# A graph layer on one core: the first four tiles' adjacency scanned ahead of the table of rows, and the table's loads and stores issued by GpSimd

## The chip, the cores and the metric

The kernel runs on one core of a Trainium2 chip. A core has five engines with instruction queues of their own: TensorE (PE in the profile; PEld is its loading of weights), VectorE (DVE), ScalarE (ACT), GpSimd (POOL) and SyncE (SP). Each engine takes its instructions in the order that was fixed before the run. Transfers between memory and the core are issued from the queues of SP, ACT and POOL and are carried by 16 DMA engines. The metric is the device time of one execution in microseconds (us), and the time of a kernel is the median of its runs.

## The reference, cut to what matters

There are 4096 nodes with 128 features (`x`) and an adjacency of 4096 x 4096 integers, with about 64 neighbours per node. Layer 0 is graph attention with 8 heads; layer 1 takes quantiles over the neighbours.

```python
def _L0_gnn_ref(nodes, adj, W, a1, a2, W1, b1, gamma, beta):
    Wh = jnp.einsum('nd,hde->hne', nodes, W)
    f1 = jnp.einsum('hnd,hd->hn', Wh, a1)
    f2 = jnp.einsum('hnd,hd->hn', Wh, a2)
    e = jax.nn.leaky_relu(f1[:, :, None] + f2[:, None, :], negative_slope=ALPHA)
    mask = (adj > 0)[None, :, :]
    att = jnp.where(mask, e, jnp.float32(-9000000000000000.0))
    att = jax.nn.softmax(att, axis=-1)
    h = jnp.einsum('hnm,hmd->hnd', att, Wh)
    h = jax.nn.elu(h)
    cat = jnp.transpose(h, (1, 0, 2)).reshape(N, NHEADS * DIM)
    x = jax.nn.elu(cat @ W1 + b1)
    out = _layernorm(nodes + x, gamma, beta)
    return out

def _L1_gnn_ref(x, A, W, b):
    ...
    keep = mask & ~remove
    n_keep = keep.sum(axis=1)
    vals = jnp.where(keep[:, :, None], x[None, :, :], big)
    svals = jnp.sort(vals, axis=1)
    w_q = jnp.asarray(1.0 / len(QUANTILES), x.dtype)
    for q in QUANTILES:
        idx = jnp.maximum(jnp.ceil(q * n_keep).astype(jnp.int32) - 1, 0)
        picked = jnp.take_along_axis(svals, idx[:, None, None], axis=1)[:, 0, :]
        agg = agg + w_q * picked
    ...
```

## The kernel before

The 4096 nodes are 32 tiles of 128 rows, and the tiles are grouped into six blocks of 4, 4, 6, 6, 6 and 6. The kernel uses the sparsity: it finds each node's list of neighbours and gathers only those rows. Three kinds of work make up the first stage.

**The front** (class `Front`) turns the adjacency into lists. `scan` loads a tile's adjacency in quarters of 128 x 1024 integers (L365, issued by SP, three buffers `a_i`), ACT checks each quarter for negative values (L367) and turns it into zeros and ones (L374), and PE packs these into words (L376, `ps_words`). `first` makes keys from the words (L389, DVE) and drains them, largest eight at a time, in 13 rounds of `MAX8` and `MATCH_REPLACE8` (`drain8`, L182 and L184). `second` and a last `drain8` finish the lists of a batch of tiles. `place` sorts the nodes of a block by the number of neighbours (result `pos_i`, L505) and POOL scatters the lists to memory (L526, `rows_d`). `pieces` cuts all of this into pieces that the main function calls up with `advance(n)`; the open pieces of a block do not count. The first piece scans tile 0. The piece of tile 0 scans tile 1 and drains tile 0; the piece of tile 1 scans tiles 2 and 3 together and drains tile 1; the pieces of tiles 2 and 3 drain these.

**The table** (`table`) writes a row for every node to memory (`xf_d`): its 128 features, then 8 + 8 numbers for the heads. It loads `w`, `x` in four parts, and `a2` and `a1` copied to all partitions; DVE multiplies and reduces `a` with `w` to `wa` (L250, L251); PE transposes `x` (L138) and ACT copies the transposed blocks out (L139); 32 products with `wa`, which show as 64 matmuls (L254), make the numbers of the heads, and ACT copies them out (L255). Four stores (L257) write the table. Its on-chip memory is a pool that is closed when the function returns.

**The gathers** (`gat`). Behind the table `gat` opens pools of its own and loads its constants (L802 to L810); DVE fills two small rows of padding (L813, stored by L814) and makes small selection tiles (L819 to L825). `load(u)` then gathers the table's rows of the neighbours for half a tile (L886, POOL) with the lists that `place` scattered (read back at L842 and L847); `load(0)` first runs all pieces through the placing of block 0. Attention, projections and normalisation of one tile after the other follow, with `advance(2)` behind each half tile, and the new rows go to memory (L1094).

The second stage (`sparse`) gathers these rows (L1549) and sorts them on DVE (L1584, L1585).

The program is written in one order, but the order on each engine is made by a scheduler before the run: it goes by the order of the program as priority and takes a later instruction first where it expects the earlier one not to be ready. So instructions of the front stand among those of the table. An instruction whose memory is freed by a pool that was closed waits for the last use of that memory.

Of the kernel before, what the change touches and what calls it, by code (L numbers as in the profile page):

```python
# [38 lines left out]
F32 = mybir.dt.float32  # L39
# [7 lines left out]
AX = mybir.AxisListType  # L47
# [3 lines left out]
P = 128  # L51
N = 4096
D = 128
NT = N // P
H = 8
# [76 lines left out]
def transpose_all(nc, psum, out, blocks, ident):  # L132

    for i in range(0, len(blocks), 4):
        ps = psum.tile([P, 4, P], F32, name="ps_tr")
        n = len(blocks[i : i + 4])
        for j in range(n):
            nc.tensor.transpose(ps[:, j, :], blocks[i + j], ident)  # L138
        nc.scalar.copy(  # L139
            out[:, i * P : (i + n) * P], ps[:, :n, :].rearrange("p a b -> p (a b)")  # L140
        )
# [79 lines left out]
    return wf, base  # L221


def table(tc, nc, c, x, w, a1, a2, xf_d):

    with tc.tile_pool(name="ta", bufs=1) as tp, tc.tile_pool(
        name="ta_ps", bufs=2, space=PSUM
    ) as psum:
        w_sb = tp.tile([P, H, D], F32, name="w_ta")
        nc.scalar.dma_start(out=w_sb, in_=w.rearrange("h d e -> d h e"))  # L230
        pad = tp.tile([1, XF], F32, name="pad_x")
        nc.gpsimd.memset(pad, 0.0)
        nc.gpsimd.memset(pad[:, D : D + H], -BIG)
        nc.scalar.dma_start(out=xf_d[0:1, :], in_=pad)
        xf = tp.tile([P, NT, XF], F32, name="xf")
        for i in range(4):
            nc.scalar.dma_start(
                out=xf[:, ts(i, 8), :D],
                in_=x[ts(i, 1024), :].rearrange("(t p) d -> p t d", p=P),
            )  # L240
        xT = tp.tile([P, N], F32, name="xT_ta")
        transpose_all(nc, psum, xT, [xf[:, t, :D] for t in range(NT)], c["idf"])
        wa = tp.tile([P, 2 * H], F32, name="wa_ta")
        for i, a in enumerate((a2, a1)):
            abc = tp.tile([P, H, D], F32, name="abc_ta", bufs=2)
            nc.scalar.dma_start(
                out=abc.rearrange("p h e -> p (h e)"),
                in_=a.rearrange("h e -> (h e)").partition_broadcast(P),
            )
            nc.vector.tensor_mul(abc, abc, w_sb)  # L250
            nc.vector.reduce_sum(wa[:, ts(i, H)], abc, axis=AX.X)  # L251
        ps_f = psum.tile([P, NT, 2 * H], F32, name="ps_fa", bufs=1)
        for t in range(NT):
            nc.tensor.matmul(ps_f[:, t, :], xT[:, ts(t, P)], wa, start=True, stop=True)  # L254
        nc.scalar.copy(xf[:, :, D:], ps_f)  # L255
        for i in range(4):
            nc.scalar.dma_start(  # L257
                out=xf_d[1 + i * 1024 : 1 + (i + 1) * 1024, :].rearrange(
                    "(t p) d -> p t d", p=P
                ),  # L260
                in_=xf[:, ts(i, 8), :],
            )
# [494 lines left out]
def gat(tc, nc, c, x, adj, xf_d, meta_d, order_d, flag_d, w, a1, a2, w1, b1, gamma, beta, x1_d):  # L757
# [22 lines left out]
    with ExitStack() as ctx:  # L780
# [3 lines left out]
        def advance(count):  # L784
            while todo and count > 0:
                name, piece = todo.pop(0)
                piece()
                count -= name != "open"
# [4 lines left out]
                advance(1)  # L793

        advance(1)
        table(tc, nc, c, x, w, a1, a2, xf_d)
        one = ctx.enter_context(tc.tile_pool(name="ga1", bufs=1))
        tp = ctx.enter_context(tc.tile_pool(name="ga2", bufs=2))
        rowp = ctx.enter_context(tc.tile_pool(name="ga3", bufs=6))
        psum = ctx.enter_context(tc.tile_pool(name="ga_ps", bufs=1, space=PSUM))  # L800
        w_sb = one.tile([P, H, D], F32, name="w_ga")
        nc.scalar.dma_start(out=w_sb, in_=w.rearrange("h d e -> d h e"))  # L802
        w1_sb = one.tile([P, H, D], F32, name="w1_ga")
        nc.scalar.dma_start(out=w1_sb, in_=w1.rearrange("(h e) o -> e h o", e=D))
        b1_sb = one.tile([P, 1], F32, name="b1_ga")
        nc.scalar.dma_start(out=b1_sb, in_=b1.rearrange("(o k) -> o k", k=1))
        bc = {}
        for name, src in (("gamma", gamma), ("beta", beta)):
            bc[name] = one.tile([P, D], F32, name=f"{name}_ga")
            nc.scalar.dma_start(out=bc[name], in_=src.partition_broadcast(P))  # L810
        for row, value in PADS:
            pad = one.tile([1, D], F32, name="pad", bufs=2)
            nc.vector.memset(pad, value)  # L813
            nc.scalar.dma_start(out=x1_d[row : row + 1, :], in_=pad)  # L814


        small = front.small[:, max(BLOCKS) * NC :]
# [286 lines left out]
        e, _ = probabilities(0, held[0], f1s[0])  # L1104
        going = []
        zT = None
        for u in range(2 * NT):
# [6 lines left out]
            if u + 1 < 2 * NT:  # L1114
                with ExitStack() as order:
                    for ins in behind:
                        order.enter_context(tc.issue_after(ins))
                    e, behind = probabilities(u + 1, held[u + 1], f1s[(u + 1) // 2])
# [912 lines left out]
def gnn(tc, x, adj, w, a1, a2, w1, b1, gamma, beta, lw, lb, out):  # L2031
    nc = tc.nc
    with ExitStack() as ctx:
        dram = ctx.enter_context(tc.tile_pool(name="dram", bufs=1, space=DRAM))
        xf_d = dram.tile([N + 1, XF], F32, name="xf_d")
        x1_d = dram.tile([N + len(PADS), D], F32, name="x1_d")
        meta_d = dram.tile([N, MW], I32, name="meta_d")
        order_d = dram.tile([N, 1], I32, name="order_d")
        flag_d = dram.tile([1, 1], I32, name="flag_d")

        keep = ctx.enter_context(tc.tile_pool(name="keep", bufs=1))
        c = constants(nc, keep)
        gat(tc, nc, c, x, adj, xf_d, meta_d, order_d, flag_d, w, a1, a2, w1, b1, gamma, beta, x1_d)
        other = nc.values_load(flag_d[0:1, 0:1], min_val=0, max_val=1)
        with tc.If(other > 0) as cmp:
            general(tc, nc, c, x, adj, w, a1, a2, w1, b1, gamma, beta, lw, lb, x1_d, out)
        with cmp.Else():
            sparse(tc, nc, c, x1_d, meta_d, order_d, lw, lb, out)
# [36 lines left out]
```

## Time and profile before

| | us |
|---|---|
| median of 3 runs | 8008.65 |
| lowest, highest | 8007.93, 8008.86 |
| profiled execution, its own time | 8009.1 |
| its span in the trace | 8007.3 |
| POOL busy, share of the span | 4407.1, 55% |
| DVE busy, share of the span | 5869.6, 73% |
| first gather of the table's rows starts | 179.2 |
| first gather of the second stage starts | 3244.0 |

The page divides the span into 40 slices of 200 us and shows the busy share of each engine as a digit in tenths. Lines of groups read: line, engine, operation, out<-in with shapes, count, then busy time and mean ns of one, then the engine's idle time just before them and what ended it. Lines of the timeline begin with the start and the duration; what stands in brackets is the idle time before and its releaser. Lines of waits read: what waited, for what, then us in total, times, longest.

### The profile page before, as it was taken

To read this page: it belongs to the slowest core of one execution; us is meant where nothing else is said; L and a number is where in the kernel's file an instruction comes from. 1 tells how busy PE (TensorE), PEld (TensorE's weight loads), DVE (VectorE), ACT (ScalarE), POOL (GpSimd) and SP (SyncE) were. 2 spreads that over 40 slices of the span, in tenths; PEclk is the share of its full clock that TensorE was granted. 3 is DMA by queue.
4 is the path that set the end of the run, shared out by engine and by line. 5 is a ranking of instruction groups with operands and counts; after the bars stand their busy time and mean duration, and the time that the engine had idled before them with its cause. 6 is when DMAs were issued, how large, how long until landed. Compare 5 with 4: busy or idle time off the path is not lost. (4 is left out here: it accounts for less than half of the span.)

```text
span 8007.3 us, 29926 instructions
## 1 busy us (share of the span) xinstructions
PE 1005.5 (13%) x5587; PEld 841.1 (11%) x5587; DVE 5869.6 (73%) x9452; ACT 2152.7 (27%) x2120; POOL 4407.1 (55%) x4564
## 2 busy tenths in 40 slices
PE   3233323322222322100000000000000000000000
PEld 1222222222222222000000000000000000000000
DVE  6555556555222222399889999999988999999999
ACT  5021202100000000133333333333333333333333
POOL 1777777777777776645435353635445444554500
PEclk9766666666566665555555555555555555555555
DMA  6232424222222222111101010101111011111100
GB/s 186 60 101 75 113 62 117 60 56 52 51 56 56 56 56 52 44 31 39 33 26 37 26 39 26 42 24 38 30 29 36 25 29 30 37 34 27 34 1 1
DMA packets 222575, 385.09 MB, mean 48 GB/s; under 512 B 121637, under 2 KB 133416, under 8 KB 222376
## 3 DMA queue, kind: packets, MB, share of 16 engines
q0 software_dynamic: 145664, 305.55, 16.1%
q1 hardware_dynamic: 64258, 70.19, 2.9%
q10 hardware_dynamic: 12454, 7.34, 0.3%
q14 instruction: 153, 1.25, 0.1%
q8 instruction: 46, 0.75, 0.0%
HBM read 372.47 MB, written 10.31 MB: 48 GB/s over the span
## 5 line engine op out<-in xcount | busy, mean ns | idle before, releaser
L1549 POOL DMA_INDIRECT rows<-x_d,info x2078 | 2037.5, 981 | 2055.4 <-DVE agg L1632 1040.5
L886 POOL DMA_INDIRECT nb<-xf_d,ids x2250 | 2139.8, 951 | 698.1 <-issue 662.6
L1583 ACT COPY low<-rows 128x2048 f32<-128x2048 f32 (+9 forms) x1009 | 1548.2, 1551 | 2552.2 <-DVE rows L1585 2210.8
L1584 DVE TENSOR_TENSOR rows<-low,rows 128x2048 f32<-128x2048 f32 (+9 forms) x1009 | 1877.3, 1885 | 210.1 <-ACT low L1583 207.0
L1585 DVE TENSOR_TENSOR rows<-low,rows 128x2048 f32<-128x2048 f32 (+9 forms) x1009 | 1875.4, 1883 | 2.7
L962 DVE TENSOR_TENSOR e<-nb,ps_small 128x144 f32<-128x144 f32 (+8 forms) x166 | 43.4, 264 | 1313.6 <-DMA nb<-xf_d,ids 1248.0
L1008 PE MATMUL ps_z<-spread,nb 128*128 128x128 f32 x4500 | 615.5, 305 | 769.4 <-DVE spread L1001 748.2
L1008 PEld LDWEIGHTS ps_z<-spread,nb 128*128 128x128 f32 x4500 | 604.4, 220 | 803.1 <-DVE spread L1001 381.0
L1639 PE MATMUL low<-idf,com 128*128 128x128 f32 x32 | 15.2, 474 | 4704.3 <-DVE rows L1585 3839.5
L970 ACT ACTIVATE ps_e<-e 128x256 f32<-128x256 f32 (+4 forms) x64 | 26.1, 408 | 1939.0 <-DVE e L962 1854.3
L1639 PEld LDWEIGHTS low<-idf,com 128*128 128x128 f32 x32 | 5.8, 181 | 4713.6 <-DVE rows L1585 3535.3
L1001 DVE TENSOR_TENSOR spread<-e,ps_small 128x1152 f32<-128x1152 f32 (+4 forms) x312 | 342.8, 1107 | 87.5 <-PE ps_z L1008 85.0
L1646 POOL DMA_INDIRECT out<-o,info x32 | 39.8, 1243 | 506.3 <-DVE o L1645 500.5
L1583 ACT COPY low_s<-rows 128x256 f32<-128x256 f32 (+3 forms) x321 | 144.8, 470 | 397.7 <-DVE rows L1584 238.1
L367 ACT ACTIVATE nz<-a_i 128x1024 bf16<-128x1024 int32 x128 | 134.4, 1051 | 233.1 <-DMA a_i<-in_adj 191.1
L182 DVE MAX8 k<-key 128x8 f32<-128x256 f32 x416 | 165.4, 411 | 0.9
L1584 DVE TENSOR_TENSOR rows<-low_s,rows 128x256 f32<-128x256 f32 (+3 forms) x321 | 156.4, 496 | 1.4 <-ACT low_s L1583 0.7
L1585 DVE TENSOR_TENSOR rows<-low_s,rows 128x256 f32<-128x256 f32 (+3 forms) x321 | 156.4, 497 | 0.4
L184 DVE MATCH_REPLACE8 key<-k,key 128x256 f32<-128x256 f32 x384 | 155.6, 407 | 0.0
L900 DVE TENSOR_TENSOR mine<-me,group 128x64 f32<-128x64 f32 x32 | 6.8, 213 | 197.2 <-DMA me<-xf_d,info 194.1
L376 PE MATMUL ps_words<-nz,pows 128*128 128x512 bf16 (+1 forms) x272 | 111.8, 568 | 289.7 <-ACT nz L374 196.0
L1587 DVE TENSOR_TENSOR rows<-rows 128x256 f32<-128x256 f32 (+8 forms) x245 | 138.4, 578 | 0.1
(222 smaller groups left out, 2502.9 us busy)
## 6 DMA issues: line engine op xcount, KB each, us to landing
a_i<-in_adj SPq DMA_DIRECT2D x128, 512.0 KB, 4.5
nb<-xf_d,ids POOLq DMA_INDIRECT x2250
rows<-x_d,info POOLq DMA_INDIRECT x2078
xf_d<-xf ACTq DMA_DIRECT2D x4, 576.0 KB, 7.5
xf<-in_x ACTq DMA_DIRECT2D x4, 512.0 KB, 7.9
meta_d<-rowdata_k SPq DMA_DIRECT2D x4, 324.0 KB, 4.0
abc_ta<-in_L_gnn_a ACTq DMA_DIRECT2D x2, 512.0 KB, 7.3
w_ga<-in_L_gnn_W ACTq DMA_DIRECT2D x2, 512.0 KB, 4.9
```

Of the source, the lines that this page charges most:

```text
L182: nc.vector.max(out=top, in_=work)
L184: nc.vector.match_replace(out=work, in_to_replace=top, in_values=work, imm_value=gone)
L367: nc.scalar.activation(nz[:, j, :], a_i, AF.Relu, scale=-1.0, accum_out=self.negative[:, k : k + 1],)
L376: nc.tensor.matmul(ps_w[:, :m, :], self.pows[:, 4 * i + b, :], nz[:, :m, ts(b, NG1)], start=i + b == 0, stop=i + b == 6,)
L886: gather = nc.gpsimd.indirect_dma_start(out=rows[:, at + i, :], out_offset=None, in_=xf_d, in_offset=bass.IndirectOffsetOnAxis(ap=ids[:, k ...
L1001: last = nc.vector.tensor_tensor(spread[:, :m], e[:, at : at + m, :].unsqueeze(2).to_broadcast(shape), own.unsqueeze(1).unsqueeze(3).to_br ...
L1008: product = nc.tensor.matmul(ps_z[:, g, :], rows[:, k + i0 + i, :D], spread[:, i].rearrange("p j h -> p (j h)"), start=i0 + i == 0, stop=i ...
L1549: nc.gpsimd.indirect_dma_start(out=row, out_offset=None, in_=x1_d, in_offset=bass.IndirectOffsetOnAxis(ap=info[:, col : col + 1], axis=0),)
L1583: nc.scalar.copy(packed, lows)
L1584: nc.vector.tensor_tensor(lows, packed, highs, op=ALU.min)
L1585: nc.vector.tensor_tensor(highs, packed, highs, op=ALU.max)
L1587: nc.vector.tensor_tensor(lows, lows, highs, op=ALU.min)
```

## The change

In `table`, all transfers are issued by POOL in place of ACT, in the order `w`, `a2`, `a1`, the four parts of `x`, the row of padding; the stores of the table too. The tiles `abc` are loaded at the start. A function `between` is called behind the loads; `gat` passes `advance(2)`, so the pieces of tiles 0 and 1 stand there in program order: the scan of tile 1, the drains of tile 0, the scan of tiles 2 and 3, the drains of tile 1. The steps on `a` (DVE) now stand ahead of the transposes. In `gat`, the loads of the constants and the stores of the two rows of padding are issued by POOL; the memsets of L813 stay on DVE.

```diff
-def table(tc, nc, c, x, w, a1, a2, xf_d):
+def table(tc, nc, c, x, w, a1, a2, xf_d, between):
...
-        w_sb = tp.tile([P, H, D], F32, name="w_ta")
-        nc.scalar.dma_start(out=w_sb, in_=w.rearrange("h d e -> d h e"))
         pad = tp.tile([1, XF], F32, name="pad_x")
         nc.gpsimd.memset(pad, 0.0)
         nc.gpsimd.memset(pad[:, D : D + H], -BIG)
-        nc.scalar.dma_start(out=xf_d[0:1, :], in_=pad)
+        w_sb = tp.tile([P, H, D], F32, name="w_ta")
+        nc.gpsimd.dma_start(out=w_sb, in_=w.rearrange("h d e -> d h e"))
+        wa = tp.tile([P, 2 * H], F32, name="wa_ta")
+        abcs = []
+        for a in (a2, a1):
+            abc = tp.tile([P, H, D], F32, name="abc_ta", bufs=2)
+            nc.gpsimd.dma_start(
+                out=abc.rearrange("p h e -> p (h e)"),
+                in_=a.rearrange("h e -> (h e)").partition_broadcast(P),
+            )
+            abcs.append(abc)
         xf = tp.tile([P, NT, XF], F32, name="xf")
         for i in range(4):
-            nc.scalar.dma_start(
+            nc.gpsimd.dma_start(
                 out=xf[:, ts(i, 8), :D],
                 in_=x[ts(i, 1024), :].rearrange("(t p) d -> p t d", p=P),
             )
+        nc.gpsimd.dma_start(out=xf_d[0:1, :], in_=pad)
+        between()
+        for i, abc in enumerate(abcs):
+            nc.vector.tensor_mul(abc, abc, w_sb)
+            nc.vector.reduce_sum(wa[:, ts(i, H)], abc, axis=AX.X)
         xT = tp.tile([P, N], F32, name="xT_ta")
         transpose_all(nc, psum, xT, [xf[:, t, :D] for t in range(NT)], c["idf"])
-        wa = tp.tile([P, 2 * H], F32, name="wa_ta")
-        for i, a in enumerate((a2, a1)):
-            abc = tp.tile([P, H, D], F32, name="abc_ta", bufs=2)
-            nc.scalar.dma_start(
-                out=abc.rearrange("p h e -> p (h e)"),
-                in_=a.rearrange("h e -> (h e)").partition_broadcast(P),
-            )
-            nc.vector.tensor_mul(abc, abc, w_sb)
-            nc.vector.reduce_sum(wa[:, ts(i, H)], abc, axis=AX.X)
...
         for i in range(4):
-            nc.scalar.dma_start(
+            nc.gpsimd.dma_start(
                 out=xf_d[1 + i * 1024 : 1 + (i + 1) * 1024, :].rearrange(
...
         advance(1)
-        table(tc, nc, c, x, w, a1, a2, xf_d)
+        table(tc, nc, c, x, w, a1, a2, xf_d, lambda: advance(2))
...
-        nc.scalar.dma_start(out=w_sb, in_=w.rearrange("h d e -> d h e"))
+        nc.gpsimd.dma_start(out=w_sb, in_=w.rearrange("h d e -> d h e"))
...
-        nc.scalar.dma_start(out=w1_sb, in_=w1.rearrange("(h e) o -> e h o", e=D))
+        nc.gpsimd.dma_start(out=w1_sb, in_=w1.rearrange("(h e) o -> e h o", e=D))
...
-        nc.scalar.dma_start(out=b1_sb, in_=b1.rearrange("(o k) -> o k", k=1))
+        nc.gpsimd.dma_start(out=b1_sb, in_=b1.rearrange("(o k) -> o k", k=1))
...
-            nc.scalar.dma_start(out=bc[name], in_=src.partition_broadcast(P))
+            nc.gpsimd.dma_start(out=bc[name], in_=src.partition_broadcast(P))
...
-            nc.scalar.dma_start(out=x1_d[row : row + 1, :], in_=pad)
+            nc.gpsimd.dma_start(out=x1_d[row : row + 1, :], in_=pad)
```

## The prediction

> **What bounds the kernel now.** I read the slices of the page first, then the waits of GpSimd (POOL) in the stretch where it is busiest, then the first 180 us instruction by instruction.
>
> ```profile
> DVE  6555556555222222399889999999988999999999
> POOL 1777777777777776645435353635445444554500
> ```
> ```profile
> L886 POOL DMA_INDIRECT nb<-xf_d,ids x2250 | 2139.8, 951 | 698.1 <-issue 662.6
> L1584 DVE TENSOR_TENSOR rows<-low,rows 128x2048 f32<-128x2048 f32 (+9 forms) x1009 | 1877.3, 1885 | 210.1 <-ACT low L1583 207.0
> ```
>
> A slice is 200 us. From slice 2 to slice 16 POOL sits at 0.7: 2250 gathers of table rows (L886), 0.95 us each plus 0.3 us "issue" ahead of each, so 1.25 us a gather. From slice 17 DVE sorts the lists at 0.9 and is the bound to the end. The sort reads rows that the first stage wrote, so the two follow each other. The waits of POOL from 170 to 3260 us say whether anything stops the first stage:
>
> ```profile
> POOL nb L886 <- issue: 662.6, 2174, 0.3
> POOL rows_d L526 <- DVE pos_i L505: 165.7, 1, 165.7
> POOL x_d L1094 <- DVE s L1091: 45.3, 2, 40.6
> POOL x_d L1094 <- DMA x_d<-s,info: 14.8, 9, 2.0
> ```
>
> One wait stands out, 165.7 us in one piece: POOL does nothing until DVE has placed the first block of four tiles. What the kernel can win at its head is therefore won one for one at its end: first gather at 179.20, everything behind it 8007.3 - 179.2 = 7828.1 us. The head itself:
>
> ```profile
> 20.55 0.42 DVE L389 SCALAR_TENSOR_TENSOR key<-ps_words,iota_g 128x256 f32<-128x256 f32 x1 [15.99 <-PE ps_words L376]
> ...
> 60.38 0.31 DVE L813 MEMSET pad<- 1x128 f32 x2 [21.93 <-DMA xf_d<-xf]
> ...
> 66.59 0.42 DVE L389 SCALAR_TENSOR_TENSOR key<-ps_words,iota_g 128x256 f32<-128x256 f32 x1 [5.23 <-PE ps_words L376]
> ```
> ```profile
> 87.18 0.75 DVE L389 SCALAR_TENSOR_TENSOR key<-ps_words,iota_g 128x256 f32<-128x256 f32 x2 [7.90 <-PE ps_words L376]
> ```
> ```profile
> DVE key L389 <- PE ps_words L376: 29.1, 3, 16.0
> DVE pad L813 <- DMA xf_d<-xf: 21.9, 1, 21.9
> ```
>
> (Timeline, then waits of DVE in the first 180 us.) DVE starts tile 0 at 20.55, tile 1 at 66.59, tiles 2 and 3 at 87.18; between them it stands 21.9 us until the table's stores have landed (the pad of L813 lies in memory that the table's pool frees), 5.2 and 7.9 us for the scans. From 87.18 on it is busy without a break to pos_i, so 179.20 - 87.18 = 92.0 us from tiles 2 and 3 to the first gather. ACT, which makes the scans, has the same holes:
>
> ```profile
> ACT xf L255 <- PE ps_fa L254: 14.8, 1, 14.8
> ...
> ACT nz L367 <- DMA a_i<-in_adj: 10.2, 13, 1.1
> ACT nz L374 <- DMA w_ga<-in_L_gnn_W: 10.1, 1, 10.1
> ```
>
> The copy L255 waits for the table's matmuls and the load of w_ga for the stores' landing, both with scans queued behind.
>
> **The change, part by part.**
>
> *Scans ahead of the table.* Undisturbed, ACT takes four quarters in 9.33 us (activations of L367 start at 76.84 and 86.17). Sixteen quarters from 6.41 are 37.3 us, with the 16 copies of pows (3.3 us) 47.0; the last activation of tiles 2 and 3 ended 1.95 us before their key (85.23 to 87.18), so the key could start at 48.9. The transfers bound it too: 16 quarters of 0.52 MB and the loads of w, a and x (3.7 MB) are 12.1 MB, at 236 GB/s (the rate of 0 to 20 us, DMA share 0.78) 51 us. I take 50. DVE is ready: tiles 0 and 1 take 12.7 us each (66.59 to 79.3), 20.55 + 25.4 = 46. The four DVE steps of L250 and L251 (4.8 us) fit into its idle time before 20.55 if w and a have landed, otherwise they cost up to 4.8 here. Gain if nothing else holds DVE: 87.2 - 50 = **37 us**.
>
> *The issues leave ACT.* ACT spent about 17 us issuing (w 0.46, x 4.6, a 2.6, pads 1.1, stores 5.0, w_ga to beta 3.2) and the 10.1 us wait for w_ga; both are inside the 37 us. On POOL the waiting costs nothing as long as its first scatter comes late: behind the stores POOL has w_ga, w1_ga and five small ones, at most 2 x 7.9 + 5 x 1.25 = 22 us, and the scatter comes over 80 us after the pad. That cover is what hides them.
>
> *What a plain transfer costs on POOL.* The trace has none. Nearest is the gather, 128 rows in 0.95 us. A load of x or w or a store of xf_d has 1024 rows. If the cost is per instruction it is 1.25 us with its issue; if per row 8 x 0.95 + 0.3 = 7.9 us. I take the middle, 4.5, since the gather has the same row length (544 against 576 bytes) but eight times fewer rows. x's last load is then issued at about 27 us (low end 11, high end 44) and lands 7.9 us later, the rows' own figure. At the high end transposes placed among the scans hold these up some 10 us.
> The Trainium skill, "DMA: Bandwidth & Descriptors", section "Anatomy of one DMA — SWDGE (gpsimd) path", calls descriptor generation small, with many descriptors emitted before the added cost shows. By that the low end holds and the 13 us that I charge below for late stores would be nothing, the time of rival A; no run shown has a transfer of more than 128 rows on this queue.
>
> *The wait at L813 stays.* The pads' memsets are still on DVE, still in memory that the table frees, and they still stand ahead of first(2) in program order. Which drains DVE does before them depends on the scheduler: in the trace it filled first(0) in ahead of L813, because that was ready earlier. So what is late next is the stores' landing. The table: eight copies of xT (0.58 us) and 64 matmuls (13.8 us in a row). If the copies go into ACT's waits for a_i (0.8 us each), L255 comes at about 50; if all wait for the scans, 47.0 + 8 x 0.87 + 13.8 = 68. I take 58. Four stores of 4.5 us and 7.5 us landing (the page's figure for xf_d): 58 + 18 + 7.5 = **83.5**; ends 50 + 5 + 7.5 = 62.5 and 68 + 31.6 + 7.5 = 107.
> DVE reaches L813 somewhere in the drains of tiles 2 and 3, 25 us long (87.18 to 112). The order is fixed before the run, by when the scheduler expects the stores. I assume that it expects the chain that I do but the price per instruction: 58 + 5 + 7.5 = 70.5, so 20.5 us into the drains. DVE then stands 83.5 - 70.5 = 13 us.
> The skill's "SBUF — State Buffer", section "SBUF: two separate sides", speaks against the change: a GpSimd transfer cannot write its descriptors while DVE runs a two-port operation. Here the 2250 gathers have a median of 0.944 us and a maximum of 2.03 with DVE half busy, so no run shown bears it out; by it the four stores would each be held by up to a 1.2 us operation, 5 us in all, 7990.
>
> *Sum.* -37 + 13 = -24. The holes of 5.2 and 7.9 us are inside the 37. The profiled execution ran 8009.1 us with a span of 8007.3; its span becomes 7983.3, its own time 7985.1, and as the median of the runs, 8008.65, is 0.45 below it, the predicted time is **7984.6 us**.
>
> **Rivals.**
>
> *A, the pads never hold DVE* (stores land before it gets there, or the pads are queued behind the second drains): 8008.65 - 37 = 7971. For it: the low end, 62.5, is within the 25 us of drains from 50. Against: it needs both the low price and an early L255.
>
> *B, the wait replaces the wait* (the pads ahead of tiles 2 and 3): first gather at 83.5 + 92 = 175.5, 4 us less, 8005. For it: pads come first by program order, and the trace has them ahead of first(1). Against: scans now outrank the table on ACT.
>
> *C, slower.* The mechanism of B with stores at the price per row: x late, L255 at 68, landing 107, first gather at 199, 8028. It decides from a landing at 103 us with nothing of tiles 2 and 3 drained. Against: both ends at once.
>
> *D, the change doesn't do it*: the scheduler puts transposes and their copies among the scans as before, since it reorders (the pad of L813 behind first(0)); scans end near 65, stores land by then, gain 87 - 65 less some of DVE's work on L250: about 20, 7989. This lies in the forecast's own range; I count it there.
>
> **How the numbers follow.** Forecast 0.45, with an own range of 7975 to 7999: DVE stands between 3 us (stores at 2 us each, 58 + 8 + 7.5 = 73.5) and 27 us (7.9 us each). A 0.27, B 0.2, C 0.08. The range 7968 to 8010 holds A, B and the forecast and leaves out C and gains over 40 us, about a tenth. A measurement can tell 0.2% here, 16 us: faster means under 7992.6. That is all of A and 0.31 of the forecast's 0.45 (up to 21 us of standing), so 0.58; C gives slower 0.07, with 0.01 of it under the bound; the rest, 0.35, is the same.
>
> **What would show it.** Key of tiles 2 and 3 near 50 (over 60: loads or transposes hold ACT). POOL's plain transfers of 1024 rows near 4.2 us: 1 us or 8 us moves me to A or towards B and C. An idle time of DVE ahead of L813, released by the stores of xf_d, of about 13 us, with drains of tiles 2 and 3 on both sides. First gather near 155, and from there to the end 7828 us; if that part differs by over 5 us, the claim that the head passes one for one is wrong.

## The result, and the profile after

| | before | changed |
|---|---|---|
| median (7 runs each), us | 8009.34 | 7983.64 |
| lowest and highest, us | 8007.93, 8011.82 | 7981.56, 7986.67 |
| span of the profiled execution, us | 8007.3 | 7984.9 |
| first gather of the table's rows, us | 179.2 | 155.0 |
| from there to the end, us | 7828.1 | 7829.9 |

The ratio is 0.9968 with a 95% interval of 0.9956 to 0.998: faster by 25.7 us, of which the trace shows 24.2 ahead of the first gather. The changed kernel's lines stand 6 further down: L813 is now L819, L255 is L261, L389 is L395, L886 is L892.

The slices of the page of the changed kernel, and its largest group:

```profile
DVE  7465556564222222399889999999988999999999
ACT  5020212100000000133333333333333333333333
POOL 2777777777777776645535353535445444554500
...
L892 POOL DMA_INDIRECT nb<-xf_d,ids x2250 | 2142.4, 952 | 697.9 <-issue 653.7
```

Nothing changed behind the head: the same 2250 gathers at 0.95 us and 0.3 us each, the same sort. The head on DVE and on POOL (timeline of the changed kernel: start, duration, and in brackets the idle time before and its releaser):

```profile
31.63 0.40 DVE L395 SCALAR_TENSOR_TENSOR key<-ps_words,iota_g 128x256 f32<-128x256 f32 x1
...
53.26 0.75 DVE L395 SCALAR_TENSOR_TENSOR key<-ps_words,iota_g 128x256 f32<-128x256 f32 x2 [7.59 <-PE ps_words L382]
...
64.01 0.74 DVE L182 MAX8 k<-key 128x8 f32<-128x256 f32 x2
71.35 0.30 DVE L819 MEMSET pad<- 1x128 f32 x2 [6.60 <-ACT nz L373]
...
81.79 0.42 DVE L395 SCALAR_TENSOR_TENSOR key<-ps_words,iota_g 128x256 f32<-128x256 f32 x1 [2.24 <-PE ps_words L382]
```
```profile
5.17 3.54 POOL L247 DMA_DIRECT2D xf<-in_x  x4
8.69 0.54 POOL L251 DMA_DIRECT2D xf_d<-pad_x  x1
57.36 3.56 POOL L263 DMA_DIRECT2D xf_d<-xf  x4 [48.13 <-ACT xf L261]
71.50 0.89 POOL L808 DMA_DIRECT2D w_ga<-in_L_gnn_W  x1 [10.58 <-DMA xf_d<-xf]
...
155.01 0.99 POOL L892 DMA_INDIRECT nb<-xf_d,ids  x1 [4.35 <-DMA ids<-rows_d]
```

Tile 1 starts on DVE at 31.6 in place of 66.6, tiles 2 and 3 at 53.3 in place of 87.2. DVE still stands at the pads, 6.6 us in the middle of the drains of tiles 2 and 3. The trace puts that wait down to an activation, but POOL's load of w_ga, which goes into memory of the same closed pool, is released by the stores of xf_d at the same moment, 71.5; with the pads in memory of their own (pads_free, below) the wait is gone. A hole that the kernel before did not have follows: 2.2 us until the words of tile 4.

The stretches of 20 us say what the transfers did (busy time of each engine, then the granted TensorE clock, the DMA share and GB/s; 0 to 20 and 60 to 80 us, changed kernel):

```profile
0.00:20.00 20.00, 1.91 (x9) 0.95 (x10) 8.03 (x87) 11.86 (x29) 7.83 (x19) 1.00 0.90 302
...
60.00:80.00 20.00, 5.71 (x13) 1.75 (x13) 12.91 (x55) 12.58 (x19) 5.30 (x9) 0.50 0.96 294
```

The loads go out at once from POOL and meet the adjacency in the first 20 us: DMA share 0.90 at 302 GB/s against 0.78 at 236 before. The stores meet it again at 0.96.

### The profile page after: what moved, and what is told of

Same layout as the page of the kernel before. It is cut to its first block, busy times and chain, and to the rows that moved or that the text cites. A ratio compares the mean times of both kernels' runs of the same rounds, so it can differ in the third digit from the quotient of the medians.

```text
span 7984.9 us, 29931 instructions
## 1 busy us (share of the span) xinstructions
PE 993.2 (12%) x5587; PEld 829.9 (10%) x5587; DVE 5867.9 (73%) x9452; ACT 2151.3 (27%) x2120; POOL 4427.5 (55%) x4583
## 5 line engine op out<-in xcount | busy, mean ns | idle before, releaser
L892 POOL DMA_INDIRECT nb<-xf_d,ids x2250 | 2142.4, 952 | 697.9 <-issue 653.7
L1652 POOL DMA_INDIRECT out<-o,info x32 | 39.6, 1237 | 506.1 <-DVE o L1651 500.3
## 6 DMA issues: line engine op xcount, KB each, us to landing
xf<-in_x POOLq DMA_DIRECT2D x4, 512.0 KB, 10.5
```

What stands on the lines that cost most here:

```text
L892: gather = nc.gpsimd.indirect_dma_start(out=rows[:, at + i, :], out_offset=None, in_=xf_d, in_offset=bass.IndirectOffsetOnAxis(ap=ids[:, k ...
```

## The experiments

They ran on two other chips, on which the kernel before took 8653.1, 8613.2 and 8606.1 us (first four runs, next four, last two). There the stretch of the gathers takes some 600 us longer and executions of one kernel differ by 17 to 50 us, so I read the head from each trace and times only against the kernel before in the same runs. The head is nearly the same on these chips: in hold_before, below, the key of tiles 2 and 3 comes at 87.20, and the changed kernel has its first gather at 152.7 (after_again) against 155.0. So 2 us between the traces of two chips say nothing by themselves. Steadier is the stretch from the key of tiles 2 and 3 to the first gather, 101.8 us in the changed kernel on the first chip and 101.2 in after_again.

**The order alone (order_only).** All transfers back on ACT:

```diff
-            nc.gpsimd.dma_start(
+            nc.scalar.dma_start(
                 out=xf[:, ts(i, 8), :D],
...
-        nc.gpsimd.dma_start(out=w_sb, in_=w.rearrange("h d e -> d h e"))
+        nc.scalar.dma_start(out=w_sb, in_=w.rearrange("h d e -> d h e"))
```

> The changed kernel with every transfer of the table and the constants issued by ACT again; only the order (scans of tiles 1 to 3 ahead of the table) is kept. Theory (order and issue each free ACT of one of its two waits): ACT pays some 8 us of issuing ahead of the scans, so the key of tiles 2 and 3 comes at 58 to 63 against 53.3 in the changed kernel, and the wait for w_ga moves behind the scans, where only tiles 4 and 5 feel it; first gather at 160 to 170 against 155.0 and 179.2, time 7988 to 7999. Rival 1 (only the issue counts, ACT's wait for w_ga is what cost): first gather at 172 or later, time over 8001. Rival 2 (only the order counts): first gather 155 to 158.

First gather 157.4, ratio 0.9968 (0.9953 to 0.9983). The key of tiles 2 and 3 came at 64.2, a little later than the theory's 58 to 63, yet the first gather falls into the range of rival 2. From key to gather it took 93.2 us, in the changed kernel 101.8: the pads cost 1.9 us in place of 6.6, tile 4's words held nobody, and 43 of the largest-eight steps of keys stood ahead of pos_i in place of 50. The timeline of ACT (order_only) has a reason for the late key, a stop of 8.2 us behind the loads of x, and the landing of the table:

```profile
32.33 1.06 ACT L373 ACTIVATE nz<-a_i 128x1024 bf16<-128x1024 int32 x1 [8.24 <-DMA xf<-in_x]
...
65.73 0.59 ACT L261 COPY xf<-ps_fa 128x512 f32<-128x512 f32 x1 [2.73 <-PE ps_fa L260]
66.35 5.11 ACTq L263 DMA_DIRECT2D xf_d<-xf  x4
77.89 0.38 ACTq L808 DMA_DIRECT2D w_ga<-in_L_gnn_W  x1
```

The table lands 6.5 us later than in the changed kernel (77.9 against 71.4), but the key comes 10.9 us later, so less is left to wait for at the pads. The stores need 11.6 us from the end of the copy to their landing (66.3 to 77.9), and 13.2 in the kernel before (47.2 to 60.4). From POOL they need 14.3 (57.1 to 71.4): POOL issues them in 3.6 us and not 5.1, and they land no sooner. The other traffic differs too (DMA share 0.67 from 60 to 80 us here, 0.96 in the changed kernel), so what the queue alone does to the landing is not shown.

**The issue alone (issue_only).** The call behind the loads does nothing:

```diff
-        table(tc, nc, c, x, w, a1, a2, xf_d, lambda: advance(2))
+        table(tc, nc, c, x, w, a1, a2, xf_d, lambda: None)
```

> The changed kernel without the pieces called behind the loads, so that the scans of tiles 1 to 3 stand behind the table in program order again; all transfers stay on GpSimd. Theory: ACT no longer waits 10.1 us for w_ga, nor issues for 17 us, so tile 1's key, at 66.6 before, comes at about 45 to 50 and that of tiles 2 and 3 near 65 to 72; DVE may stand at the pads until the stores land near 55; first gather at 158 to 170. Rival 1 (only the issue counts): 153 to 157, as the changed kernel or earlier, since the table is done sooner. Rival 2 (only the order counts): 175 to 180.

First gather 159.6, ratio 0.9965 (0.9947 to 0.9982), as the theory had it; tile 1 on DVE at 38.2 (even earlier than expected), tiles 2 and 3 at 67.2. The idle times of DVE (timeline of issue_only):

```profile
48.01 0.30 DVE L819 MEMSET pad<- 1x128 f32 x2 [3.50 <-DMA xf_d<-xf]
...
67.24 0.76 DVE L395 SCALAR_TENSOR_TENSOR key<-ps_words,iota_g 128x256 f32<-128x256 f32 x2 [12.27 <-PE ps_words L382]
```

Each half alone brings the first gather 20 to 22 us forward, both 24 (26.5 in after_again). They do not add, because both take away the same thing, the two waits of ACT that stand ahead of the scans of tiles 2 and 3 in the kernel before, 14.8 us for the table's matmuls and 10.1 for w_ga. In order_only both come behind these scans, and the first is 2.7 us long; in issue_only the first is 1.7 us and the second is gone from ACT.

**Only the constants on GpSimd (consts_pool).** The kernel before, with L802 to L814 issued by GpSimd as in the diff of the change.

> The kernel before, with only the constants' loads and the stores of the padding rows (from w_ga on) issued by GpSimd; table, order and its issues as before. It takes away ACT's 10.1 us wait for w_ga alone. Theory (that wait is one of two; the one for the table's matmuls, 14.8 us with scans behind it, stays): the scan of tile 1 goes on while the stores land, the keys of tiles 2 and 3 come at 74 to 80 against 87.2, first gather at 166 to 173. Rival (the wait for w_ga is all that issuing by GpSimd removed): first gather at 158 to 162, as in issue_only.

First gather 173.5, just past the theory's 173; key of tiles 2 and 3 at 81.6, past its 80; ratio 0.9982 (0.9968 to 0.9996). Without the wait for w_ga the head wins 5.7 us, not the 10.1 that ACT stood there; ACT still waits 15.6 us for the table's matmuls, and DVE stood 23.3 us at the pads. The rest of what issue_only wins must come from its other edits, the table's own loads and steps; which of them was not tried.

**The pads out of the way (pads_free).**

```diff
+        ahead = ctx.enter_context(tc.tile_pool(name="ga0", bufs=1))
         table(tc, nc, c, x, w, a1, a2, xf_d, lambda: advance(2))
...
-            pad = one.tile([1, D], F32, name="pad", bufs=2)
+            pad = ahead.tile([1, D], F32, name="pad", bufs=2)
...
-        group = one.tile([P, GR], F32, name="group")
+        group = ahead.tile([P, GR], F32, name="group")
```

(`place` and `wide` alike.)

> The changed kernel with the two rows of padding and the tiles group, place and wide in a pool that is opened ahead of the table, so DVE waits for no memory of the table there (6.6 us in the changed kernel). Theory from its trace: the hole moves. The key of tile 4 stands in DVE's order behind the drains of tiles 2 and 3 and its words came at 81.8, 2.2 us after DVE was ready; without the 6.6 us DVE gets there at about 72 and stands 8 to 9 us; first gather 153.5 to 155.5, time the same within 2 us. Rival (the wait was on the path by itself): first gather at 148 to 149, time 6 to 7 us less than the changed kernel, 7977.

```profile
53.77 0.76 DVE L395 SCALAR_TENSOR_TENSOR key<-ps_words,iota_g 128x256 f32<-128x256 f32 x2 [7.62 <-PE ps_words L382]
...
80.62 0.42 DVE L395 SCALAR_TENSOR_TENSOR key<-ps_words,iota_g 128x256 f32<-128x256 f32 x1 [3.90 <-PE ps_words L382]
```
```profile
149.43 0.98 POOL L893 DMA_INDIRECT nb<-xf_d,ids  x1 [4.32 <-DMA ids<-rows_d]
```

(Timelines of pads_free, DVE and POOL.) First gather 149.4, 5.6 us ahead of the changed kernel's profile of the first chip and 3.3 ahead of after_again's; ratio 0.9965 (0.9952 to 0.9978). From key to gather it took 95.7 us, 6.1 and 5.5 less than in these two. My theory missed: the hole ahead of tile 4's key grew from 2.2 to 3.9 us only, because DVE's order changed with the edit and steps on the lists of tiles 2 and 3 now stand ahead of that key. The wait at the pads lay on the path nearly in full; hold and hold_pads, below, show the same on one chip.

**One for one (delay).** Sixty more steps ahead of pos_i:

```diff
+        if b == 0:
+            for _ in range(60):
+                nc.vector.tensor_scalar(work, work, 1.0, None, op0=ALU.mult)
         num = small("num")
```

> The changed kernel with 60 more steps of DVE in the placing of block 0 (a list times 1.0, 0.36 us each by the row of L447, in a chain), ahead of pos_i. Theory (the head passes one for one): the first gather comes 17 to 36 us later than 155.0, and the span grows by the same number within 4 us. Rival (part of the gather stage has slack, the 3.1 us that the changed kernel lost between first and last gather being its sign): the span grows by less than two thirds of what the first gather moves.

First gather 191.1, 36.1 us later than 155.0; from key to gather 140.5 us, 38.7 more than in the changed kernel, past the theory's 36. The sixty steps are not all of it: they are busy for 22.9 us, and 78 of the largest-eight steps of keys stood ahead of pos_i in place of 50, since the order changed with the edit. As a test of what a later head does to the end this does no harm. Ratio 1.0011 (1.0000 to 1.0021). The changed kernel did not run in this group, so the mark is pads_free: its head is 41.7 us shorter and its median 39.6 us less (8623.5 against 8663.1). The rival's two thirds would be 28. From first gather to end the profiles have 8467.4 and 8475.5 us, so my 4 us are missed by these two executions, 8.1 us apart, on a chip where executions of one kernel differ by more.

**The changed kernel again (after_again).**

> The changed kernel itself once more, as the mark for the others on the same chip. Theory: first gather at 154 to 156 and 23 to 27 us less than the kernel before, whatever that kernel's time is on the chip. On a chip where the gathers wait for other things than POOL, a rival says that the head is hidden and the difference falls under 15 us.

First gather 152.7, ahead of the theory's 154 to 156: the key of tiles 2 and 3 came at 51.5, and the wait at the pads was 5.6 us. Median 8591.6 against 8613.2, 21.5 less, ratio 0.9958 (0.9939 to 0.9978). The theory's 23 was missed by 1.5 us, less than these executions differ; the gain did not fall under the rival's 15. This is the mark for the next three.

**Tile 4 held back (hold).** The keys of tiles 4 to 7 issue behind pos_i of block 0:

```diff
+        with ExitStack() as order:
+            if START[1] <= t < START[2]:
+                order.enter_context(self.tc.issue_after(self.placed))
             nc.vector.scalar_tensor_tensor(
```

> The changed kernel with the keys of tiles 4 to 7 held on DVE until the places of block 0 (pos_i) are made; until now 23 of their largest-eight steps with their replacements, about 21 us busy, stood on DVE between the key of tiles 2 and 3 and pos_i. Theory (what lies between that key and the first gather is DVE's work and not block 0's own chain): the hole of 2.2 us ahead of tile 4's key and most of the 21 us go, less up to 10 us in which the held steps covered waits of the chain; first gather at 132 to 142 against 155, time 13 to 23 us less than the changed kernel. Rival 1 (they only filled gaps of the chain): first gather at 150 or later. Rival 2 (block 1 then comes late): first gather as in the theory, but POOL stands for block 1 and the time is no more than 5 us less.

Between the key of tiles 2 and 3 and the first gather, DVE in the changed kernel also drains tiles 4 and 5: 24 of their `MAX8` steps stood ahead of pos_i in after_again, none here (timelines of hold, DVE and POOL):

```profile
129.59 0.17 DVE L514 CAST pos_i<-pos 128x4 int32<-128x4 f32 x1
129.67 0.74 DVE L398 SCALAR_TENSOR_TENSOR key<-ps_words,iota_g 128x256 f32<-128x256 f32 x2
```
```profile
130.05 1.04 POOL L537 DMA_INDIRECT rows_d<-rowdata,pos_i  x1 [56.69 <-DVE pos_i L514]
...
139.37 0.98 POOL L897 DMA_INDIRECT nb<-xf_d,ids  x1 [4.46 <-DMA ids<-rows_d]
```

First gather 139.4, 13.3 us ahead of after_again, as the theory expected; median 16.1 less (8575.6), ratio to before 0.9952 (0.9936 to 0.9968). The runs of the two overlap (8552 to 8588 and 8550 to 8597), so the gain is shown in the head and not by the time alone. Of the 21 us of held work and 2.7 us of hole some 10 did not come back. They were not waits that the trace shows: DVE is busy for 59.4 of the 60.6 us between the pads and pos_i in hold. The rounds of the drain give the size. In the kernel before a round of tile 0 alone begins every 0.98 us, and a round of tiles 2 and 3 together every 1.44 us (timeline of DVE):

```profile
21.01 0.43 DVE L182 MAX8 k<-key 128x8 f32<-128x256 f32 x1
...
21.99 0.43 DVE L182 MAX8 k<-key 128x8 f32<-128x256 f32 x1
...
87.85 0.74 DVE L182 MAX8 k<-key 128x8 f32<-128x256 f32 x2
...
89.29 0.74 DVE L182 MAX8 k<-key 128x8 f32<-128x256 f32 x2
```

A round that runs beside another tile's costs 0.46 us more, not 0.98. At that price 24 rounds are 11 us, an estimate from these rows; hold_before, below, wins 10.8.

**Held, and the pads free (hold_pads).**

> The keys held as in the run hold, and the rows of padding and the selection tiles in memory of their own as in pads_free. Theory: both holes are on the path, so the 5.6 us that pads_free gained in the first gather come on top; first gather at 126 to 137, 4 to 7 us ahead of hold, time 18 to 30 us less than the changed kernel. Rival: DVE, no longer delayed, meets another wait (words of tiles 2 and 3 or the read-back of the lists) and the two do not add, first gather within 2 us of hold.

First gather 133.7, another 5.7 us, which is what pads_free won; the two add. Median 8561.6, 51.6 less than the kernel before and 30 less than the changed one, ratio 0.9944 (0.9927 to 0.9961). It has the shortest head and the lowest time of its group. Against the changed kernel the gain is shown in the head, 19.0 us; the intervals of the two ratios overlap.

**Four pieces ahead (four_ahead).** `advance(4)` in place of `advance(2)`.

> The changed kernel with four pieces behind the loads in place of two, so that the scan of tiles 4 and 5 and the drains of tiles 2 and 3 also outrank the table. Theory (ACT's order sets the table's end): L261 comes 5 to 15 us later than 56.5, the pads stand behind the drains of tiles 2 and 3 but the stores land later too, at 77 to 87 against 71.4; the wait at the pads is 0 to 8 us and the first gather comes within 5 us of 155. Rival (the more scans ahead the better): pads without a wait and first gather under 149.

First gather 148.4: the rival's number, but not its reason. L261 came at 60.3 and the stores landed at 75.7. Against after_again, on the same chip, both are some 7 us later, which lies in the theory's 5 to 15 for L261. DVE still stood 3.5 us at the pads (5.6 there), and the hole ahead of tile 4 shrank to 0.5 us (2.7 there). The two waits got 4.3 us shorter together, and the first gather came 4.3 us earlier; the theory had not counted the hole. Ratio 0.9958 (0.9943 to 0.9973), from after_again not to be told.

**The hold on the kernel before (hold_before).** The diff of hold, nothing else.

> The kernel before, with the keys of tiles 4 to 7 held until block 0 is placed and nothing else; 24 of their largest-eight steps stood ahead of pos_i there, as many as in the changed kernel. Theory (the held work is a cost of its own, apart from the change): first gather 10 to 15 us earlier, 164 to 169, time 8 to 18 us less. Rival (it only shows once the scans are ahead): 174 or later.

First gather 168.4, median 20.5 less, ratio 0.9978 (0.9965 to 0.999). The gain of the hold does not need the change; its size in the head is 10.8 us here and 13.3 there.

## Why the prediction was right

The time (7984.6 forecast, 7983.64 measured) and the first gather (155, 155.0) agree closer than the steps do. Point by point:

- **The bound.** POOL waits for block 0, and the head passes to the end. The changed kernel's head is 24.2 us shorter and its span 22.4; from first gather to end it is 7829.9 us against 7828.1, within the 5 us that the prediction allowed. In the other groups the median follows the first gather, at a distance. Against 179.2 and the kernel before they moved by -22 and -23 us (order_only), -20 and -26 (issue_only), -30 and -30 (pads_free), +12 and +10 (delay), -27 and -22 (after_again), -40 and -38 (hold), -46 and -52 (hold_pads), -31 and -41 (four_ahead), -6 and -14 (consts_pool), -11 and -21 (hold_before). One for one is shown to 2 us on the first chip, and to some 10 us on the others.
- **Scans ahead of the table**, key of tiles 2 and 3 at 50: it was 53.3, so 33.9 us and not 37. I had taken 51 from the transfers at 236 GB/s and settled between it and 48.9. The waits of ACT (first 180 us) and the longest of those ahead of the key:

```profile
ACT nz L373 <- DMA a_i<-in_adj: 28.2, 17, 4.9
...
ACT xf L261 <- PE ps_fa L260: 3.2, 1, 3.2
```
```profile
17.84 1.06 ACT L373 ACTIVATE nz<-a_i 128x1024 bf16<-128x1024 int32 x1 [4.57 <-DMA a_i<-in_adj]
```

  ACT waited 28.2 us for adjacency, 10.2 before; but only 9.7 of the 28.2 lie ahead of the key at 53.3. The longest of these, 4.6 us, ends at 17.8 us, in the wake of the loads of x; that the loads cause it was not tried by itself. Another part is what rival D expected: six of the eight copies of xT, 0.56 to 0.57 us each, stood among the scans. The two longest waits of the 180 us, 4.9 us each, end behind the key: one at 70.1, in the wake of the stores, among the scans of tiles 4 and 5, whose words DVE then waits for in the hole of 2.2 us, the other at 84.7. The 14.8 us wait for the table's matmuls is 3.2 us and stands behind the scans of tiles 2 and 3, as the forecast assumed.
- **A plain transfer on POOL**, 4.5 us between 1.25 and 7.9: the term that was most wrong. Four stores take 3.56 us, 0.89 each, below my low end, as no 0.3 us of issue stands between them. 1024 rows cost POOL no more than 128 gathered ones. The Trainium skill's "DMA: Bandwidth & Descriptors", section "Anatomy of one DMA — SWDGE (gpsimd) path", says that many descriptors go out before their cost shows; this trace agrees, with 0.89 us for 1024 rows.
- **The landing**, 7.5 us behind the last issue: it was 10.5 (60.9 to 71.4), so the low price of the issue was partly paid back. L261 came at 56.5 (58 forecast), the stores landed at 71.4 (83.5). The same page of the Trainium skill, section "Issuing engines are not separate DMA queues", says that another queue saves the issue only; this case agrees in so far as the landing shows no gain: the stores landed 13.9 us (issue_only) to 14.9 (four_ahead) behind their copy from POOL, and 11.6 (order_only) to 14.6 (consts_pool) from ACT.
- **The wait at the pads**: the mechanism held, with drains on both sides. The size was 6.6 us for 13. Two errors met: the stores landed 12 us earlier than forecast, and the pads stood 11.5 us into the drains (53.3 to 64.8), not 20.5. The 25 us that the prediction gives these drains are too long as well: in the kernel before the thirteen rounds of tiles 2 and 3 take 18.6 us (87.2 to 105.8), so a pad 20.5 us in would have stood behind them. That the wait was on the path is shown by pads_free (5.5 to 6.1 us less from key to gather) and by hold_pads against hold (5.7).
- **What I did not have**: the 2.2 us hole ahead of tile 4's key, and that the 92.0 us between key and first gather, carried over whole, hold 10.8 us of drains of other tiles (hold_before). The sum measured: -33.9 + 6.6 + 2.2 + 0.9 = -24.2, where the 0.9 is what remains, nearly all of it the steps of the pads and selection tiles, which now stand behind the key. Against -37 + 13 the misses are +3.1, -6.4 and +3.1: they cancel to 0.2 us, and that is luck.
- **The rivals.** A needs the landing ahead of the pads: 71.4 against 64.8, missed by 6.6 us. B and C needed dear stores and the pads ahead of tiles 2 and 3; neither was so. D fell with the key at 53.3 and the scans' end at 51.3 in place of 65, though copies did stand among the scans.
- The descriptor rule of the Trainium skill's "SBUF — State Buffer", section "SBUF: two separate sides", did not show: the plain transfers took 0.89 us beside DVE's drains. No run here shows whether the drains' steps are two-port operations, so the rule was not put to the test.

## What to carry to other kernels

When one engine is the bound from its first instruction on, look at what it waits for before that, and take every instruction out of the way that is not its own chain: here some 20 of 24 us came from either of two edits, another 13 from holding work that was early for no one, and 6 from giving a few small tiles memory of their own. Two edits that remove the same wait do not add; try each alone. An edit also changes the order that the scheduler makes, so count what stands ahead in each trace before a difference is put down to the edit. Here the other queue changed what issuing the stores cost, and brought no gain in the time from their copy to their landing. The wait for memory that the stores free stayed with the tiles that used it, whichever queue issued them, and went when these had a pool of their own.

## What the runs showed of the hardware that was not expected

- A transfer of 1024 rows costs POOL 0.89 us, a gather of 128 rows 0.95.
- A round of the drain takes DVE 0.98 us for one tile alone and 1.44 us for two tiles side by side.
- The granted TensorE clock is shown as 1.00 until 180 us in the kernel before, and as 0.78 and then 0.50 from 20 us on in the changed kernel. The table's matmuls do not bear this out for the kernel before (timeline of the changed kernel, then group of the kernel before):

```profile
24.84 0.96 PE L260 MATMUL ps_fa<-wa_ta,xT_ta 128*128 128x16 f32 x8
...
46.63 1.73 PE L260 MATMUL ps_fa<-wa_ta,xT_ta 128*128 128x16 f32 x8
```
```profile
L254 PE MATMUL ps_fa<-wa_ta,xT_ta 128*128 128x16 f32 x64 | 13.8, 374 | 2.1 <-DVE wa_ta L251 2.1
```

  In the changed kernel one takes 0.12 us while the clock is 1.00 (until 30 us) and 0.22 us where it is 0.50 (from 33 us on). In the kernel before all 64 take 0.22 us each, under a clock shown as 1.00. So either the clock is not as shown there, or something else held these matmuls to the same pace; which is open.
- On the other two chips the stretch from first to last gather takes 3599 us (after_again) where the first chip has 3011, with the gathers themselves at 0.95 us. PE and DVE stand there in pieces of up to 42 and 33 us that the trace puts down to "issue" and "remote" (waits in the gather stage of after_again):

```profile
PE ps_z L1014 <- issue: 740.8, 357, 42.3
POOL nb L892 <- issue: 642.9, 2085, 7.7
DVE spread L1007 <- remote: 564.5, 44, 32.9
```

  What this is stays open; nothing was tried for it. That the head still passes there is what the medians say, to some 10 us.
